# Head sums of two groups issued together, with other tile counts, in an attention stack on one Trainium2 core

## The chip, the cores and the metric

The kernel runs on one core of one Trainium2 chip. The metric is the device time of one execution in microseconds; lower is better. A core has four computing engines that run their own instruction streams and wait for each other through semaphores: TensorE (PE in the profile, its weight loads PEld), VectorE (DVE), ScalarE (ACT) and GpSimd (POOL). SyncE (SP) issues the DMAs. TensorE writes only to PSUM, which this kernel uses as eight banks of 128 partitions by 512 floats; everything else lies in SBUF.

## The reference, cut to what matters

Six attention layers (`D=6`) run over a batch of `B=8` sequences of `L=512` rows with `E=128` features and `H=16` heads of width 8; a gated feed-forward part follows. In each layer the softmax weights are averaged over the heads, a fixed decay is added, and a second softmax is taken:

```python
scores = jnp.einsum('blhd,bmhd->bhlm', q, k) * inv_sqrt_d
w_avg = jax.nn.softmax(scores, axis=-1).mean(axis=1)
new_w = jax.nn.softmax(CSCALE * w_avg + rel[None], axis=-1)
sa = jnp.einsum('blm,bme->ble', new_w, h)
h1 = _ln(h + sa, l1w, l1b)
h2 = _ln(h1, l2w, l2b)
ff = jax.nn.relu(h2 @ w1.T + b1_) @ w2.T + b2_
return (_ln(h2 + ff, l3w, l3b), None)
```

The feed-forward part at the end adds `tlin(gelu(tlin(gelu(tlin(silu(..)*..)))))` of the normalised sum to it, with weights of 512 by 512.

## The kernel before, in words

**Units and steps.** The work is a row of 48 units, one for each layer and batch element (`units`, line 202). A unit has 32 steps (`PAIRS`, line 204). Each step computes two score tiles: 128 rows (32 query rows times 4 heads) by 512 keys. Step `s` of a unit is `lc = s // 8` (a block of 128 query rows), `turn = s // 2 % 4` (four heads of the 16) and `half = s % 2`. Two steps make a `Group` (line 367): four score tiles of the same four heads, whose exponentials lie in one tile `e` of 128 x 4 x 512. The text below counts steps within a unit, 0 to 31, so groups with odd `turn` end at steps 3, 7, 11 and so on.

**One score tile** goes through three engines. TensorE multiplies it into one of six PSUM banks that are used in a ring (`ring`, line 156; `scores`, line 385, one pass in a faster 32-bit format). VectorE reduces it to the negated maximum of each row (`peak`, line 394, `top`). ScalarE takes the exponential with that maximum as bias and sums the rows on the way (`exps`, line 399, `e` and `zs`); after that the bank is free for the score tile six tiles later.

**The sum over heads.** For each group VectorE takes the reciprocal of the row sums (line 408) and GpSimd builds the weights `rp` (line 410). Then `gather` (line 417) multiplies `rp` into `e`: four matmuls, each with 128 x 32 weights and a 512 wide operand, each into its own 32 partitions of one PSUM bank `acc`. They are plain 32-bit matmuls and take two passes, so a group has eight matmul records. The four groups of one `lc` accumulate in `acc`; `mix_exp` (line 425) then reads it on ScalarE into `w`. After that come `mix_turn` (four transposes of `w`, line 432), `mix_decay` (line 437), `mix_values` (line 445) and `mix_end` (lines 453 and 454).

**The order of the work** is written out by hand. `later` maps (step, place) to functions, `at` appends one, `first` puts it ahead. In each step the loop at line 579 issues the two score matmuls, then what is pending for TensorE, then the two maxima, then what is pending for VectorE (GpSimd and DMA issues are called from there), then what is pending for ScalarE, then the two exponentials. Each engine takes its instructions in the order issued. `plan_group` (line 538) places, for a group whose second half is step `s`: `weights` in `s+2`, `gather` in `s+5` ahead of other TensorE work of that step, and for the last turn `mix_exp` in `s+5`, `mix_turn` and `mix_decay` in `s+8`, `mix_values` and `mix_end` in `s+10`. So gathers stand in every even step. The odd steps hold one other piece of TensorE work each: `po` (`mix_values`) in steps 1, 9, 17, 25; the transposes `pt_w` in steps 7, 15, 23, 31 (in step 31 also `pt_h` and `pt_u`, lines 220 and 322, which take two banks of the ring); `pk` and `pq` in 3 and 5; `pf` (`hidden`, line 336) in 11, 13, 19, 21; and `py` (`mlp_out`, line 348, sixteen short matmuls) in 27 and 29. In the steps of `py` VectorE adds the result at once (`mlp_add`, line 355).

**The end.** When the last unit's steps are done, the remaining pieces are mixed into the feed-forward part (`gated_in`, `gated`, lines 606 to 663), which runs over the eight batch elements. There `gated_in(b)` adds the input `x` on GpSimd, issues the load of the next one (line 611), and normalises into the tile `vf`; `gated(b)` writes `sil` (line 633), the hidden tiles in the pool of `e`, and `y`.

**Tiles.** Pools give a number of buffers by tag: `e` 4, `w` 2 (shared with `sil`), `wT` 2, `hT` 2 (shared with `vT`), `x` 3, `rp` 4, `acc` 1.

Of the kernel before, what the change touches and what calls it, by code (L numbers as in the profile page):

```python
# [9 lines left out]
F32 = mybir.dt.float32  # L10
# [7 lines left out]
P = 128  # L18
# [3 lines left out]
QB = 32  # L22
# [7 lines left out]
def attn_stack_then_ffn(ctx: ExitStack, tc: tile.TileContext, a: dict, out: bass.AP):  # L30
    nc = tc.nc
    ctx.enter_context(tc.manual_schedule())
    x = a["x"]
    B, L, E = x.shape
# [4 lines left out]
    LC = L // P  # L39
    FC = F // P  # L40
    HC = HID // P
    NB = P // QB
# [4 lines left out]
    wts = ctx.enter_context(tc.tile_pool(name="wts", bufs=1))  # L47
    state = ctx.enter_context(tc.tile_pool(name="state", bufs=1))
    proj = ctx.enter_context(tc.tile_pool(name="proj", bufs=2))
    epool = ctx.enter_context(tc.tile_pool(name="e", bufs=4))  # L50
    work = ctx.enter_context(tc.tile_pool(name="work", bufs=2))
    small = ctx.enter_context(tc.tile_pool(name="small", bufs=6))
    ps_big = ctx.enter_context(tc.tile_pool(name="ps_big", bufs=6, space=PSUM))
# [39 lines left out]
    x_in = {}  # L93

    def load_x(b, n):
        t = state.tile([P, LC, E], F32, tag="x", name=f"x_{n}", bufs=3)
        nc.sync.dma_start(t, x[b].rearrange("(c p) e -> p c e", p=P))
        return t

# [4 lines left out]
    def load_layer(d):  # L104
        qk = wts.tile([P, 2, E], F32, tag="wqk", name=f"wqk_{d}", bufs=2)
        nc.sync.dma_start(qk, a["wqk"][d].rearrange("t e o -> e t o"))
        w1 = wts.tile([P, F], F32, tag="w1", name=f"w1_{d}", bufs=2)
        nc.sync.dma_start(w1, a["w1t"][d])
        w2 = wts.tile([P, FC, E], F32, tag="w2", name=f"w2_{d}", bufs=2)
        nc.sync.dma_start(w2, a["w2t"][d].rearrange("(c p) e -> p c e", p=P))  # L110
        r = wts.tile([P, len(ROWS), E], F32, tag="rows", name=f"rows_{d}", bufs=2)
        nc.sync.dma_start(
            r.rearrange("p k e -> p (k e)"),
            a["rows"][d].rearrange("k e -> (k e)").partition_broadcast(P),
        )
        rows = {name: r[:, k, :] for k, name in enumerate(ROWS)}
        b2s = wts.tile([P, E], F32, tag="b2s", name=f"b2s_{d}", bufs=2)
        nc.gpsimd.tensor_tensor(b2s, rows["ln2_b"], rows["b2"], ALU.add)
        rows["b2s"] = b2s
        lay[d] = (qk, w1, w2, rows)  # L120
# [69 lines left out]
    def transpose(pt, src):  # L190

        for c in range(LC):
            nc.tensor.transpose(pt[:, c * P : (c + 1) * P], src[:, c, :], ident)  # L193

    def transposed(src, n):
        pt = one([P, L], f"pt_{n}")
        transpose(pt, src)
        return pt
# [7 lines left out]
    class Unit:  # L206
# [12 lines left out]

        def turn_h(self, pt):  # L220
            transpose(pt, self.h[:, :, 0:E])
            self.hT = work.tile([P, L], F32, tag="hT", name=f"hT_{self.n}")
            return lambda: nc.scalar.copy(self.hT, pt)

        def project_k(self):
# [141 lines left out]
    class Group:  # L367
# [38 lines left out]
        def weights(self):  # L406
            r = small.tile([P, NB], F32, tag="r", name=f"r_{self.n}")
            nc.vector.reciprocal(r, self.zs)  # L408
            self.rp = small.tile([P, NB, QB], F32, tag="rp", name=f"rp_{self.n}", bufs=4)
            nc.gpsimd.tensor_tensor(  # L410
                self.rp,
                pick.unsqueeze(1).to_broadcast([P, NB, QB]),
                r.unsqueeze(2).to_broadcast([P, NB, QB]),
                ALU.mult,
            )
# [7 lines left out]
                )  # L423

        def mix_exp(self):
            self.w = work.tile([P, LC, P], F32, tag="w", name=f"w_{self.n}")
            nc.scalar.activation(  # L427
                self.w.rearrange("p c l -> p (c l)"), acc, AF.Exp, scale=1.0 / H
            )
# [31 lines left out]
    PE_, DVE_, ACT_, RING_ = range(4)  # L461
    later = {}

    def at(step, place, fn):
        later.setdefault((step, place), []).append(fn)

    def first(step, place, fn):
        later.setdefault((step, place), []).insert(0, fn)

    def pending(step, place):  # L470
        for fn in later.pop((step, place), ()):
            fn()
# [62 lines left out]
        at(s + PAIRS + 11, DVE_, lambda: un.affine_c(0))  # L535
        at(s + PAIRS + 12, DVE_, lambda: un.affine_c(1))

    def plan_group(gr, s):

        first(s + 2, DVE_, gr.weights)  # L540
        first(s + 5, PE_, gr.gather)
        if gr.turn == STRIPS - 1:
            at(s + 5, ACT_, gr.mix_exp)
            at(s + 8, PE_, gr.mix_turn)
            at(s + 8, DVE_, gr.mix_decay)
            at(s + 10, PE_, gr.mix_values)
            at(s + 10, DVE_, gr.mix_end)
# [6 lines left out]
    def step_ring(s):  # L554
        for fn in later.pop((s, RING_), ()):
            fn()()

    for s in range(-2 * PAIRS, 0):
# [4 lines left out]
        step_rest(s)  # L563
        step_ring(s)

    for u, un in enumerate(obj):
        un.z1 = work.tile([P, LC, E], F32, tag="z1", name=f"z1_{un.n}")
        if u + 2 < B:
            x_in[u + 2] = load_x(u + 2, f"in{u + 2}")
        if un.b == 4 and un.d + 1 < D:  # L570
            load_layer(un.d + 1)
        if u == U - B:
            load_ffn()
            xs = {0: load_x(0, "out0")}
        if u + 2 < U:
            plan_before(obj[u + 2])
        plan_turns(u)
        plan_after(un)
        for pr in range(PAIRS):
            s = u * PAIRS + pr  # L580
            lc, turn, half = pr // 8, (pr // 2) % STRIPS, pr % 2
            if half == 0:
                gr = Group(un, lc, turn)
            peak, exps = gr.scores(half)
            if half == 1:
                plan_group(gr, s)
            pending(s, PE_)
            peak()
            pending(s, DVE_)
            pending(s, ACT_)  # L590
            exps()
            step_ring(s)
# [13 lines left out]
    def gated_in(b):  # L606

        xb = xs.pop(b)
        nc.gpsimd.tensor_tensor(xb, xb, hs[b][:, :, 0:E], ALU.add)
        if b + 1 < B:  # L610
            xs[b + 1] = load_x(b + 1, f"out{b + 1}")
        v = work.tile([P, LC, E], F32, tag="vf", name=f"v_{b}", bufs=1)
        ln = Norm(xb, v, f"f{b}")
        ln.stats(0, LC)
        ln.aggregate()
        ln.centre()
        ln.scale()
        yield
        vT = work.tile([P, L], F32, tag="hT", name=f"vT_{b}")
        pt = transposed(v, f"v{b}")  # L620
        nc.scalar.copy(vT, pt)  # L621
        ready[b] = (xb, vT)

    def gated(b):
        xb, vT = ready.pop(b)
        ahead = gated_in(b + 1) if b + 1 < B else iter(())
        gg = epool.tile([P, HC, L], F32, tag="e", name=f"fg_{b}")
        for o in range(HC):
            sl = slice(o * P, (o + 1) * P)
            p1, p2 = ring([P, L], f"p1_{b}_{o}"), ring([P, L], f"p2_{b}_{o}")  # L630
            nc.tensor.matmul(p1, fw1[:, sl], vT, start=True, stop=True)
            nc.tensor.matmul(p2, fw2[:, sl], vT, start=True, stop=True)
            sil = work.tile([P, L], F32, tag="w", name=f"sil_{b}_{o}")
            nc.scalar.activation(sil, p1, AF.Silu, scale=cols["f_w1s_col"][:, o : o + 1])
            nc.vector.scalar_tensor_tensor(
                gg[:, o, :], p2, cols["f_w2s_col"][:, o : o + 1], sil, ALU.mult, ALU.mult
            )
            yield
        for wt, sc, nm in ((fh1, "f_h1s_col", "h1"), (fh2, "f_h2s_col", "h2")):
            g2 = epool.tile([P, HC, L], F32, tag="e", name=f"{nm}_{b}")  # L640
            for o in range(HC):
                ph = ring([P, L], f"p{nm}_{b}_{o}")
                for c in range(HC):
                    nc.tensor.matmul(  # L644
                        ph, wt[:, c, o * P : (o + 1) * P], gg[:, c, :],
                        start=(c == 0), stop=(c == HC - 1),
                    )
                nc.scalar.activation(g2[:, o, :], ph, AF.Gelu, scale=cols[sc][:, o : o + 1])
                if (nm, o) in (("h1", HC - 1), ("h2", HC - 1)):
                    next(ahead, None)  # L650
                yield
            gg = g2
        po = ring([P, LC, E], f"fo_{b}")
        for c in range(LC):
            for k in range(HC):
                nc.tensor.matmul(  # L656
                    po[:, c, :], gg[:, k, c * P : (c + 1) * P], fw3[:, k, :],
                    start=(k == 0), stop=(k == HC - 1),
                )
        y = work.tile([P, LC, E], F32, tag="z1", name=f"y_{b}")  # L660
        nc.vector.tensor_tensor(y, po, fw3s.unsqueeze(1).to_broadcast([P, LC, E]), ALU.mult)  # L661
        nc.gpsimd.tensor_tensor(y, y, xb, ALU.add)  # L662
        nc.sync.dma_start(out[b].rearrange("(c p) e -> p c e", p=P), y)

    for _ in gated_in(0):
        pass
# [66 lines left out]
```

## Time and profile before

| | |
|---|---|
| median of three runs | 2820.88 us (2820.86 to 2822.2) |
| the profiled execution | 2825.2 us, of which the span of its instructions is 2823.4 us |
| TensorE clock granted | 0.998 of full |
| busy: PE, ACT, DVE, POOL | 2746.7, 2496.5, 2393.9, 1801.2 us |
| time from one unit's first exponential to the next one's, units 3 to 46 | 50.5 to 51.1 us, 51.0 for nearly all |
| from the first exponential of unit 47 to its last | 48.8 us |
| after the last exponential | 2823.4 - 2479.6 = 344 us |

A row of the profile gives line, engine, operation, tiles written and read, shape and count; then busy time in us and the mean of one in ns; then the idle time of the engine just before such instructions and who ended it. In a timeline the first column is the start in us, the second how long the merged row lasted; brackets hold the idle time before it. Busy time of TensorE is counted from pipelined matmuls whose ends are modelled, so the distance from one start to the next says more than a duration.

### The profile page before, as it was taken

The numbers are of one execution on the slowest core, as the hardware profiler recorded it, in microseconds if no ns is written. First come the engines' busy times: TensorE is split into PE (matmuls) and PEld (weight loads), VectorE is DVE, ScalarE is ACT, GpSimd is POOL, SyncE is SP. The second block draws the span as 40 slices with busy tenths as digits, with TensorE's granted clock in tenths as the row PEclk, the third lists the DMA queues.
The fourth block names the chain that finished last, engine by engine and source line by source line (L and its number), as shares of the span: only waits on it lengthen the run. The fifth ranks groups of instructions, "written<-read, shape, count | busy, mean of one in ns | idle before, by whom it ended". The sixth has DMA issues, their size and how long they took to land.

```text
span 2823.4 us, 51628 instructions
## 1 busy us (share of the span) xinstructions
PE 2746.7 (97%) x14944; PEld 1370.0 (49%) x14944; DVE 2393.9 (85%) x5942; ACT 2496.5 (88%) x6845; POOL 1801.2 (64%) x2205
## 2 busy tenths in 40 slices
PE   5999999999999999999999999999999999989999
PEld 2444545445454454454544545445445454445554
DVE  4999999999999999999999999999999999921110
ACT  5999999999999999999999999999999999933232
POOL 4668776776766767767677676676776767633210
PEclk9999999999999999999999999999999999999999
DMA  5555444544544445444454454454564444300000
GB/s 117 114 118 132 93 104 104 112 108 106 111 105 107 97 113 115 110 92 103 105 127 104 93 113 106 103 120 94 117 153 95 102 105 110 78 8 8 15 12 8
DMA packets 133387, 271.06 MB, mean 96 GB/s; under 512 B 39024, under 2 KB 56560, under 8 KB 133104
## 3 DMA queue, kind: packets, MB, share of 16 engines
q1 hardware_dynamic: 131808, 267.73, 42.3%
q8 instruction: 119, 1.95, 0.3%
q14 instruction: 164, 1.34, 0.2%
q10 hardware_dynamic: 1296, 0.03, 0.0%
HBM read 13.86 MB, written 2.10 MB: 6 GB/s over the span
## 4 chain that ended last, share of the span: by engine, by line
PE 47%; ACT 22%; DVE 18%; POOL 6%; issue 5%; DMA 0%; SPq 0%; POOLq 0%; ACTq 0%; DVEq 0%
ACT e L399 19%; DVE top L394 14%; PE ps L385 13%; PE acc L420 12%; PE py L348 6%; PE ph L644 6%; PE po L445 3%; PE pk L229 1%; ACT w L427 1%; POOL z L306 1%; PE pq L238 1%; POOL rs_a L178 1%; POOL z L186 1%; POOL z L181 1%; ACT g L338 1%
## 5 line engine op out<-in xcount | busy, mean ns | idle before, releaser
L399 ACT ACTIVATE e<-ps,top 128x512 f32<-128x512 f32 x3072 | 2134.5, 840 | 23.9 <-DVE top L394 20.4
L394 DVE TENSOR_REDUCE top<-ps 128x1 f32<-128x512 f32 x3072 | 1952.5, 682 | 42.9 <-PE ps L385 35.8
L385 PE MATMUL ps<-ks,qs 128*128 128x512 f32 x3072 | 1240.0, 477 | 34.2 <-ACT e L399 26.0
L399 ACT ACTIVATION_READ_ACCUMULATOR e<-ps,top 128x1 f32 x3072 | 1103.5, 359 | 0.0
L385 PEld LDWEIGHTS ps<-ks,qs 128*128 128x128 f32 x3072 | 495.4, 189 | 888.3 <-ACT e L399 661.6
L420 PE MATMUL acc<-e,rp 128*32 128x512 f32 x6144 | 819.1, 605 | 0.8 <-POOL rp L410 0.3
L410 POOL TENSOR_TENSOR rp<-pick,r 128x128 f32<-128x128 f32 x768 | 308.1, 401 | 549.8 <-DVE r L408 265.8
L420 PEld LDWEIGHTS acc<-e,rp 128*32 128x32 f32 x6144 | 121.0, 108 | 263.1 <-issue 126.5
L278 POOL TENSOR_TENSOR m<-hiq,mask 128x512 f32<-128x512 f32 x192 | 245.2, 1277 | 4.8 <-DMA qs<-m 4.8
L278 POOL TENSOR_TENSOR m<-loq,mask 128x512 f32<-128x512 f32 x192 | 245.1, 1277 | 2.6 <-DMA qs<-m 2.6
L445 PEld LDWEIGHTS po<-h,wT 128*128 128x128 f32 x1536 | 201.0, 191 | 18.9 <-DVE wT L437 1.5
L445 PE MATMUL po<-h,wT 128*128 128x129 f32 x1536 | 202.7, 275 | 0.7 <-DVE wT L437 0.7
L336 PE MATMUL pf<-uT,w 128*128 128x512 f32 x384 | 195.8, 591 | 0.0
L348 PEld LDWEIGHTS py<-w,g 128*128 128x128 f32 x1536 | 186.2, 192 | 10.9 <-ACT vT L621 1.1
L348 PE MATMUL py<-w,g 128*128 128x128 f32 x1536 | 186.9, 275 | 0.8 <-ACT vT L621 0.8
L338 ACT ACTIVATE g<-pf,b_col 128x512 f32<-128x512 f32 x192 | 168.2, 876 | 2.2 <-PE pf L336 2.2
L661 DVE TENSOR_TENSOR y<-fo,fw3s 128x512 f32<-128x512 f32 x8 | 5.5, 692 | 175.8 <-PE fo L656 175.8
L427 ACT ACTIVATE w<-acc 128x512 f32<-128x512 f32 x192 | 134.2, 699 | 22.6 <-PE acc L420 22.6
L662 POOL TENSOR_TENSOR y<-y,x_out 128x512 f32<-128x512 f32 x8 | 10.1, 1265 | 199.7 <-DVE y L661 199.7
L408 DVE RECIPROCAL r<-zs 128x4 f32<-128x4 f32 x768 | 130.9, 170 | 5.7 <-ACT e L399 0.3
L437 DVE TENSOR_TENSOR wT<-pt_w,decay 128x512 f32<-128x512 f32 x192 | 126.9, 661 | 4.5 <-PE pt_w L193 4.2
L355 DVE TENSOR_TENSOR z<-py,z 128x256 f32<-128x256 f32 x96 | 40.8, 425 | 105.3 <-PE py L348 105.3
(97 smaller groups left out, 2637.3 us busy)
## 6 DMA issues: line engine op xcount, KB each, us to landing
qs<-m SPq DMA_DIRECT2D x1536, 128.0 KB, 2.4
ks<-hik SPq DMA_DIRECT2D x384, 64.0 KB, 2.0
ks<-lok SPq DMA_DIRECT2D x384, 64.0 KB, 2.0
rows<-in_rows SPq DMA_DIRECT2D x6, 448.0 KB, 5.1
x_in<-in_x SPq DMA_DIRECT2D x8, 256.0 KB, 3.1
x_out<-in_x SPq DMA_DIRECT2D x8, 256.0 KB, 3.1
out<-y SPq DMA_DIRECT2D x8, 256.0 KB, 2.4
w<-in_w1t SPq DMA_DIRECT2D x6, 256.0 KB, 2.9
```

What stands on the lines that cost most here:

```text
L278: nc.gpsimd.tensor_tensor(m[:, lc - 2 * two], part.unsqueeze(2).to_broadcast([P, NB, PER_STRIP, QB]), mask.unsqueeze(1).to_broadcast([P, N ...
L336: nc.tensor.matmul(pf, w1[:, f * P : (f + 1) * P], self.uT, start=True, stop=True)
L338: return lambda: nc.scalar.activation(self.g[:, f, :], pf, AF.Relu, bias=cols["b1_col"][:, k : k + 1])
L348: nc.tensor.matmul(self.py[:, k, :], self.g[:, f, c * P : (c + 1) * P], w2[:, f, :], start=(f == 0), stop=(f == FC - 1),)
L385: nc.tensor.matmul(ps[s], qs[:, nb * P : (nb + 1) * P].bitcast(F32R), un.ks[:, i, :].bitcast(F32R), start=True, stop=True,)
L394: nc.vector.tensor_reduce(top[s], ps[s], AX.X, ALU.max, negate=True)
L399: nc.scalar.activation(self.e[:, nb, :], ps[s], AF.Exp, bias=top[s], accum_out=self.zs[:, nb : nb + 1],)
L410: nc.gpsimd.tensor_tensor(self.rp, pick.unsqueeze(1).to_broadcast([P, NB, QB]), r.unsqueeze(2).to_broadcast([P, NB, QB]), ALU.mult,)
L420: nc.tensor.matmul(acc[nb * QB : (nb + 1) * QB, :], self.rp[:, nb, :], self.e[:, nb, :], start=(self.turn == 0), stop=(self.turn == STRIPS ...
L427: nc.scalar.activation(self.w.rearrange("p c l -> p (c l)"), acc, AF.Exp, scale=1.0 / H)
L445: nc.tensor.matmul(self.po, self.wT[:, c, :], self.unit.h[:, c, 0 : E + 1], start=(c == 0), stop=(c == LC - 1),)
L644: nc.tensor.matmul(ph, wt[:, c, o * P : (o + 1) * P], gg[:, c, :], start=(c == 0), stop=(c == HC - 1),)
```

## The change

The gathers of two neighbouring groups (turns 0 and 1, or 2 and 3) are held back until the second one's place, and are issued there one behind the other: sixteen matmul records in steps 0, 4, 8 and so on, none in steps 2, 6, 10. `mix_exp` moves from `s+5` to `s+6`. The pool of `e` gets five tiles, `rp` six; `w`, `hT` (with `vT`) get one, `x` two. `v` of the end takes the tag `m0`, `sil` the tag `wT`. The inputs of the end are loaded two at the start of the last layer, then each one after the output of the element two before it.

```diff
-    epool = ctx.enter_context(tc.tile_pool(name="e", bufs=4))
+    epool = ctx.enter_context(tc.tile_pool(name="e", bufs=5))
...
-        t = state.tile([P, LC, E], F32, tag="x", name=f"x_{n}", bufs=3)
+        t = state.tile([P, LC, E], F32, tag="x", name=f"x_{n}", bufs=2)
...
-            self.hT = work.tile([P, L], F32, tag="hT", name=f"hT_{self.n}")
+            self.hT = work.tile([P, L], F32, tag="hT", name=f"hT_{self.n}", bufs=1)
...
-            self.rp = small.tile([P, NB, QB], F32, tag="rp", name=f"rp_{self.n}", bufs=4)
+            self.rp = small.tile([P, NB, QB], F32, tag="rp", name=f"rp_{self.n}", bufs=6)
...
-            self.w = work.tile([P, LC, P], F32, tag="w", name=f"w_{self.n}")
+            self.w = work.tile([P, LC, P], F32, tag="w", name=f"w_{self.n}", bufs=1)
...
-    def plan_group(gr, s):
+    def plan_group(pair, gr, s):
         first(s + 2, DVE_, gr.weights)
-        first(s + 5, PE_, gr.gather)
+        pair.append(gr)
+        if len(pair) == 2:
+            two = tuple(pair)
+            pair.clear()
+            first(s + 5, PE_, lambda: [x.gather() for x in two])
         if gr.turn == STRIPS - 1:
-            at(s + 5, ACT_, gr.mix_exp)
+            at(s + 6, ACT_, gr.mix_exp)
             at(s + 8, PE_, gr.mix_turn)
...
-            xs = {0: load_x(0, "out0")}
+            xs = {b: load_x(b, f"out{b}") for b in range(2)}
...
-        if b + 1 < B:
-            xs[b + 1] = load_x(b + 1, f"out{b + 1}")
-        v = work.tile([P, LC, E], F32, tag="vf", name=f"v_{b}", bufs=1)
+        v = work.tile([P, LC, E], F32, tag="m0", name=f"v_{b}", bufs=1)
...
-        vT = work.tile([P, L], F32, tag="hT", name=f"vT_{b}")
+        vT = work.tile([P, L], F32, tag="hT", name=f"vT_{b}", bufs=1)
...
-            sil = work.tile([P, L], F32, tag="w", name=f"sil_{b}_{o}")
+            sil = work.tile([P, L], F32, tag="wT", name=f"sil_{b}_{o}")
...
         nc.sync.dma_start(out[b].rearrange("(c p) e -> p c e", p=P), y)
+        if b + 2 < B:
+            xs[b + 2] = load_x(b + 2, f"out{b + 2}")
```

More of the change, by code (lines that the diff above doesn't have):

```diff
@@ L564, in attn_stack_then_ffn @@
         step_ring(s)
+    pair = []
     for u, un in enumerate(obj):
@@ L585, in attn_stack_then_ffn @@
             if half == 1:
-                plan_group(gr, s)
+                plan_group(pair, gr, s)
             pending(s, PE_)
```

## The prediction, made before the result was known

> **What bounds the kernel now.** I read the page's busy times and costliest groups first.
>
> ```profile
> PE 2746.7 (97%) x14944; PEld 1370.0 (49%) x14944; DVE 2393.9 (85%) x5942; ACT 2496.5 (88%) x6845; POOL 1801.2 (64%) x2205
> ...
> L399 ACT ACTIVATE e<-ps,top 128x512 f32<-128x512 f32 x3072 | 2134.5, 840 | 23.9 <-DVE top L394 20.4
> L394 DVE TENSOR_REDUCE top<-ps 128x1 f32<-128x512 f32 x3072 | 1952.5, 682 | 42.9 <-PE ps L385 35.8
> L385 PE MATMUL ps<-ks,qs 128*128 128x512 f32 x3072 | 1240.0, 477 | 34.2 <-ACT e L399 26.0
> L420 PE MATMUL acc<-e,rp 128*32 128x512 f32 x6144 | 819.1, 605 | 0.8 <-POOL rp L410 0.3
> L427 ACT ACTIVATE w<-acc 128x512 f32<-128x512 f32 x192 | 134.2, 699 | 22.6 <-PE acc L420 22.6
> L355 DVE TENSOR_TENSOR z<-py,z 128x256 f32<-128x256 f32 x96 | 40.8, 425 | 105.3 <-PE py L348 105.3
> ```
>
> PE looks like the bound at 97%, but those shares mix the attention stack with the end, where ACT and DVE have little to do. Hence one unit of 51 us by itself, from the busy times by stretches (columns: window, span, PE, PEld, DVE, ACT, POOL, clock, DMA share, GB/s):
>
> ```profile
> 1411.25:1462.24 50.99, 50.46 (x293) 25.27 (x292) 48.93 (x123) 49.98 (x142) 36.38 (x45) 1.00 0.54 126
> ```
>
> Three engines stand within 2 us of the period. Next, PE's timeline from step 24 to step 30 of that unit:
>
> ```profile
> 1446.23 0.49 PE L385 MATMUL ps<-ks,qs 128*128 128x512 f32 x1 [0.17 <-ACT e L399]
> 1446.65 1.06 PE L420 MATMUL acc<-e,rp 128*32 128x512 f32 x8
> 1447.65 0.73 PE L385 MATMUL ps<-ks,qs 128*128 128x512 f32 x2
> 1448.22 1.05 PE L445 MATMUL po<-h,wT 128*128 128x129 f32 x8
> 1449.03 0.71 PE L385 MATMUL ps<-ks,qs 128*128 128x512 f32 x2
> 1449.67 1.07 PE L420 MATMUL acc<-e,rp 128*32 128x512 f32 x8
> 1450.66 0.73 PE L385 MATMUL ps<-ks,qs 128*128 128x512 f32 x2
> 1451.23 1.95 PE L348 MATMUL py<-w,g 128*128 128x128 f32 x16
> 1452.93 0.70 PE L385 MATMUL ps<-ks,qs 128*128 128x512 f32 x2
> 1453.57 1.06 PE L420 MATMUL acc<-e,rp 128*32 128x512 f32 x8
> 1454.56 0.73 PE L385 MATMUL ps<-ks,qs 128*128 128x512 f32 x2
> 1455.13 1.95 PE L348 MATMUL py<-w,g 128*128 128x128 f32 x16
> 1456.83 0.71 PE L385 MATMUL ps<-ks,qs 128*128 128x512 f32 x2
> ```
>
> The first row waits for ACT to free a bank: until step 24 the ring holds PE back. From there to step 30 PE never waits. ACT and DVE in the same stretch:
>
> ```profile
> 1454.70 0.60 ACT L427 ACTIVATE w<-acc 128x512 f32<-128x512 f32 x1 [0.47 <-PE acc L420]
> ...
> 1458.23 0.69 ACT L399 ACTIVATE e<-ps,top 128x512 f32<-128x512 f32 x1 [0.25 <-DVE top L394]
> ```
>
> ```profile
> 1453.22 0.42 DVE L355 TENSOR_TENSOR z<-py,z 128x256 f32<-128x256 f32 x1 [0.64 <-PE py L348]
> ...
> 1457.12 0.42 DVE L355 TENSOR_TENSOR z<-py,z 128x256 f32<-128x256 f32 x1 [0.61 <-PE py L348]
> ```
>
> So a unit has two parts. From step 3 to step 27 ACT's starts follow each other without a gap: the exponentials set the pace. Around the two `py` blocks PE sets it. ACT's least time per unit, from the smallest distances between starts: 64 exponentials x 0.664 + 4 `w` x 0.478 + 4 `g` x 0.571 + `qT` 0.571, `kT` 0.587, `hT` 0.466, `uT` 0.676 = 49.0 us. DVE's, likewise (64 maxima x 0.597, the rest about 10.4), is some 48.5. Even if PE cost nothing a unit would keep 49.0 of its 51.0 us.
>
> **What the Trainium skill says.** "TensorEngine Tiling", section Tiling Modes, says that changing the tiling mode drains TensorE. The trace agrees: from the last `acc` start to the next score matmul are 522 ns, where plain passes follow each other in 429; and from a score matmul to `acc` 327, to other work 231. "TensorE: Matmul & The Clock Gate", Part 3, has tiles of one mode start about 4 ns apart; here the four of a pass start 6 to 7 ns apart, so a group costs two passes of 433 + 20 ns. The same page, in its architectural detail, calls ACT and DVE strict FIFO; the `z` rows above show it, for the maxima of the next step stand behind that wait. "Perfetto Trace Analysis", Per-engine timelines, says that a matmul's end is computed; I therefore count starts, and rows such as 0.49 are not used as costs.
>
> **The change, part by part.** *Pairing, on PE.* With a gather between steps 2 and 3 of a pair, from the second score matmul of one step to the second of the next are 327 + 453 + 20 + 522 + 338 = 1660 ns. Without one, where the trace has four score matmuls in a row, about 235 + 230 = 465. So the dropped block saves 1195, and the second group behind the first adds 2 x 453 = 906: 289 ns less PE per pair, 384 x 0.289 = 111 us in all, if PE alone set the time. No trace shows two groups in a row; it could not be under 2 x 433 and not over a separate block, so the pair gains 0 to 0.33.
>
> *Pairing, on the path.* What PE saves in steps 3 to 27 is worth nothing, since the ring stops it anyway. What counts is that one break in the supply of score tiles grows from 1.32 us (score to score) to 2.23. Take step n = 8 or 16, where PE stands at the ring, and t = 0 at the start of the second exponential of step n-3. Score matmuls that wait for the ring start 0.88 to 1.14 after it; I take 0.90, as an idle moment on ACT shortens the lag. First gather +0.43 (the distance after such a wait), then 3 x 0.453 + 0.02 + 0.522 = 1.90: the next score matmul at 3.23. Its maximum starts 0.54 later, at 3.77; DVE has been out of work since about 3.2 (with a single group it would come at 2.86, before that). Then two maxima 1.21, and in the `po` step `r` 0.085, `rw` 0.174, `z` 0.267: the maximum of step n+2 at 5.51, its exponential 0.75 later at 6.26. ACT would have been there after nine exponentials, 5.98. Loss 0.28 us, twice per unit: **+0.56**. With the ends of the lag (0.88 to 1.14, and 0.71 to 0.78 from maximum to exponential) it is 0.2 to 0.5; if DVE has a backlog, 0.
>
> *Around `py`.* From the ring-held score matmul of step 24 (1446.23) to the first of step 30 (1456.83) are 10.60 us with three groups in three blocks, steps 24, 26 and 28. With pairs in 24 and 28 it is four groups in two blocks: + 2 x 0.906 - 1.195 = +0.62. The exponentials of step 30 wait for this today (the 0.25 above), so they come 0.62 later, less about 0.20 for the shorter ring lag. After that, steps 30 to 3, a single pair in step 0 and PE 0.9 earlier at `pk`: ACT's waits there, `kT` 0.32 and two others 0.2, go, and two of about 0.2 come for the maxima behind that pair: -0.13. Together **+0.29**, ends 0 and +0.7.
>
> Per unit +0.85. Units 3 to 46 have the full load: 44 x 0.85 = **+37 us**. Units 0 to 2 and 47 I leave as they are (within 3 us).
>
> *`mix_exp` a step later.* It costs ACT the same 0.478, now behind two more exponentials (1.33) while the pair ends 0.91 later: its 22.6 us of waits mostly go, which is in the sums above. Behind it on ACT stand `g` or `qT` and the exponentials; for it waits `mix_turn` two steps on, where the ring stops PE by more. `acc` is free three steps before the next pair. Cost 0; without the ring's wait up to 0.25 a time.
>
> *Buffers.* Five `e`: the exponentials that reuse a tile come two steps behind its gather (over 2.6 us), as before; with four they would stand behind the pair. `rp` six: likewise nothing. One `w`: read in step s+8, next written in s+14, six steps or 9 us later. One `hT`: written after step 31, last read in 5, 26 steps free. Two `x`: the third was never needed at once in the stack. All 0. *The end:* the load of `x` is now behind the output of the element two before, on SP where nothing else is queued and behind GpSimd's `y`; it takes 3.1 us to land and is first used after 16 + 32 passes of 0.43, some 20 us. `v` in `m0` and `sil` in `wT` meet tiles long read. Cost 0; without that cover up to 6 x 3.1 = 19 us.
>
> **The sum.** The profiled execution took 2825.2 us (span 2823.4), 0.15% over the median of 2820.9; 2825.2 + 37 = 2862, against the median **2858 us**.
>
> **Rivals.**
> 1. *The saved switches reach the end* (faster). If DVE keeps 0.6 us of maxima in hand when a pair begins, it doesn't run dry, and the three pairs around `py` and step 0 give 3 x 0.289 = 0.87 us per unit: 45 x 0.87 = 39 us, **2782**. For it: PE at 97%, and a full ring of six tiles holds 4 us of exponentials, more than the 2.23. Against it: DVE has only what it hasn't yet reduced, and it now runs dry at two blocks that are shorter than a pair (0.64 and 0.61 before `z`). It decides at 0.6 us of backlog on DVE.
> 2. *ACT's floor* (faster still): all of ACT's 2.0 us of gaps per unit go, 45 x 2.0 = 90, **2731**. Against it: two `py` blocks and a pair still stand between steps 26 and 30.
> 3. *A wash*: the losses of steps 8 and 16 equal what the later `mix_exp` and the PE time bring: **2821**.
>
> **Chances.** Slower as worked out 0.60; same 0.10; rival 1 0.20; rival 2 0.10. Faster and slower mean more than 0.2%, about 6 us, what a measurement of this kernel can tell from none. The forecast's own range is 0 to +1.6 per unit: 2821 to 2891. Slower and faster cases both count, so the 8 in 10 reach from 2775 (rival 2 and the lower part of rival 1 left out) to 2890.
>
> **What would show it.** In the trace of after: 384 runs of sixteen `acc` records, passes 433 apart; four score matmuls in a row before each; PE busy per unit down by about 2 us where the period is not. Gaps of DVE of 0.5 us ahead of the first maximum after a pair in steps 9 and 17, gaps of ACT of 0.3 at steps 10 and 18; the exponential of step 30 about a microsecond after its predecessor. I am wrong if DVE has no such gaps, or if the period falls under 51.0. A unit of 50.1 would be rival 1, 49.0 rival 2.

## The result, and the profile after

| | before | after |
|---|---|---|
| median | 2821.19 us (2820.86 to 2822.2, 4 runs) | 2861.86 us (2861.32 to 2863.21, 4 runs) |
| ratio, 95% interval | 1 | 1.0144 [1.0127, 1.0162] |
| profiled execution, its span | 2825.2 us, 2823.4 | 2862.03 us, 2860.2 |
| granted clock | 0.998 | 0.997 |

The change makes the kernel 1.4% slower, 40.7 us by the medians, and 36.8 us between the two spans that the profile shows: the profiled execution before lies 4.0 us above its median, the one after 0.2. From the page after: the busy times, and the costliest groups.

```profile
PE 2700.5 (94%) x14944; PEld 1426.5 (50%) x14944; DVE 2376.9 (83%) x5942; ACT 2511.9 (88%) x6845; POOL 1798.2 (63%) x2205
...
L399 ACT ACTIVATE e<-ps,top 128x512 f32<-128x512 f32 x3072 | 2079.0, 729 | 77.5 <-DVE top L394 68.8
L394 DVE TENSOR_REDUCE top<-ps 128x1 f32<-128x512 f32 x3072 | 1938.8, 682 | 130.9 <-PE ps L385 126.3
L385 PE MATMUL ps<-ks,qs 128*128 128x512 f32 x3072 | 1153.9, 466 | 46.2 <-ACT e L399 36.6
L420 PE MATMUL acc<-e,rp 128*32 128x512 f32 x6144 | 740.1, 599 | 0.0
```

The instructions are the same in number. TensorE is busy for 46 us less, and the kernel is slower: PE's busy share was not what set the time. The last column has what came in its place. VectorE's maxima waited 35.8 us for score tiles before and wait 126.3 now; the exponentials waited 20.4 us for their maxima and wait 68.8. The same unit by itself, in the busy times by stretches (same columns as before):

```profile
1433.06:1484.77 51.71, 49.46 (x293) 26.46 (x293) 48.52 (x123) 50.30 (x142) 36.28 (x45) 1.00 0.53 124
```

A unit takes 51.7 us in place of 51.0. Next PE's timeline from step 24 to step 30, with pairs in steps 24 and 28:

```profile
1468.03 0.51 PE L385 MATMUL ps<-ks,qs 128*128 128x512 f32 x1 [0.17 <-ACT e L399]
1468.47 1.92 PE L420 MATMUL acc<-e,rp 128*32 128x512 f32 x16
1470.32 0.72 PE L385 MATMUL ps<-ks,qs 128*128 128x512 f32 x2
...
1471.69 1.17 PE L385 MATMUL ps<-ks,qs 128*128 128x512 f32 x4
1472.82 2.02 PE L348 MATMUL py<-w,g 128*128 128x128 f32 x16
1474.60 0.71 PE L385 MATMUL ps<-ks,qs 128*128 128x512 f32 x2
...
1479.36 1.18 PE L385 MATMUL ps<-ks,qs 128*128 128x512 f32 x4
```

The pair is there: sixteen `acc` records in a row, and four score matmuls in a row where the single group of step 26 stood. No score tile is produced from 1468.03 to 1470.32, 2.29 us (1.42 before, from 1446.23 to 1447.65). What that does to VectorE in steps 9 and 17, two excerpts of its timeline:

```profile
1445.06 0.42 DVE L247 TENSOR_SCALAR hiq<-qT 128x512 int32<-128x512 int32 x1
1445.88 1.29 DVE L394 TENSOR_REDUCE top<-ps 128x1 f32<-128x512 f32 x2 [0.39 <-PE ps L385]
...
1447.34 0.35 DVE L454 SCALAR_TENSOR_TENSOR z<-po,rw,h 128x128 f32<-128x128 f32 x1
1447.61 1.88 DVE L394 TENSOR_REDUCE top<-ps 128x1 f32<-128x512 f32 x3
...
1458.37 1.29 DVE L394 TENSOR_REDUCE top<-ps 128x1 f32<-128x512 f32 x2 [0.48 <-PE ps L385]
```

VectorE runs dry for 0.39 and 0.48 us, although it still had `hiq` to do in step 9; then `r`, `rw` and `z` stand ahead of the maxima of step 10. In step 25, behind the pair of step 24, it is dry for 0.49. Behind the pairs of steps 12 and 20 it is not idle: there the maxima start 0.85 us after their score matmuls, not the 0.54 of a VectorE that waits for them. To be dry is not yet a loss: behind step 4 VectorE is dry for 0.37 us in both kernels, but the exponentials follow their maxima by more than 2 us there, so ScalarE has work. Next ScalarE, from the last exponential of step 9 to the first of step 10 in that unit, and in step 30 (rows between are left out):

```profile
1447.46 0.80 ACT L399 ACTIVATE e<-ps,top 128x512 f32<-128x512 f32 x1
...
1448.38 0.69 ACT L399 ACTIVATE e<-ps,top 128x512 f32<-128x512 f32 x1
...
1480.76 0.69 ACT L399 ACTIVATE e<-ps,top 128x512 f32<-128x512 f32 x1 [0.96 <-DVE top L394]
```

Starts are 0.664 apart when ScalarE has work; from 1447.46 to 1448.38 it is 0.92, so 0.26 is lost. The view of idle times doesn't list it: the recorded duration (0.80) fills the distance. One has to look at starts.

**Where the time came from.** I number a unit's 64 exponentials from 0, two to a step, measure each from the start of that unit's `uT`, and take the same number of before off that of after. The difference is 0 up to exponential 3. Apart from steps 4, 12, 20 and 28, where `w` now comes behind the exponentials and no longer ahead of them, it changes at these places:

| place | what lies there | change, us |
|---|---|---|
| steps 2 and 3 | +0.11 behind the pair of step 0, then `kT` (no wait any more) | -0.23 |
| step 10 | pair of step 8 | +0.25 |
| step 18 | pair of step 16 | +0.24 |
| steps 26 to 30 | pair of step 24, both `py`, pair of step 28 | +0.46 |
| the unit | 51.71 against 50.99 | +0.72 |

Of the 0.46, 0.25 shows at step 26, as behind the other two pairs; but the exponentials of step 30 wait for PE, so the sum is set by PE's chain from step 24 to step 30.

Over the span: units 3 to 46 take 2276.3 us against 2243.6 (+32.7), units 0 to 2 150.0 against 145.7 (+4.3), unit 47 +0.9, and what lies before the first exponential and after the last -1.1. That is the 36.8.

From the list of waits after, with the columns time, times, longest:

```profile
PE pt_w L193 <- ACT g L338: 47.3, 92, 0.6
```

The waits of `kT` (10.8 us in 43 before) are gone but for the first, of 2.2, and those of `w` (22.6) have no line left. New is `pt_w`: `w` now comes ahead of `g` in the same step of ScalarE, and `pt_w` needs the one bank that `g` still reads (in step 7 it is `qT`: another 23.6 us in 46). The second experiment says what that costs.

### The profile page after: what moved, and what is told of

It is laid out like the page before. It is cut to its first block, busy times and chain, and to the rows that moved or that the text cites. A ratio compares the mean times of both kernels' runs of the same rounds, so it can differ in the third digit from the quotient of the medians.

```text
span 2860.2 us, 51679 instructions
## 1 busy us (share of the span) xinstructions
PE 2700.5 (94%) x14944; PEld 1426.5 (50%) x14944; DVE 2376.9 (83%) x5942; ACT 2511.9 (88%) x6845; POOL 1798.2 (63%) x2205
## 4 chain that ended last, share of the span: by engine, by line
ACT 35%; PE 34%; DVE 22%; issue 8%; POOL 1%; DMA 0%; SPq 0%; POOLq 0%; ACTq 0%; DVEq 0%
ACT e L399 29%; DVE top L394 17%; PE acc L420 10%; PE ps L385 7%; PE py L348 6%; PE ph L648 6%; ACT g L338 2%; ACT w L427 2%; PE po L445 1%; DVE st_b L172 1%; ACT kT L230 1%; DVE wT L437 1%; PE p L635 1%; PE p L636 1%; ACT qT L239 1%
## 5 line engine op out<-in xcount | busy, mean ns | idle before, releaser
L399 ACT ACTIVATE e<-ps,top 128x512 f32<-128x512 f32 x3072 | 2079.0, 729 | 77.5 <-DVE top L394 68.8
L394 DVE TENSOR_REDUCE top<-ps 128x1 f32<-128x512 f32 x3072 | 1938.8, 682 | 130.9 <-PE ps L385 126.3
L385 PE MATMUL ps<-ks,qs 128*128 128x512 f32 x3072 | 1153.9, 466 | 46.2 <-ACT e L399 36.6
L385 PEld LDWEIGHTS ps<-ks,qs 128*128 128x128 f32 x3072 | 527.9, 189 | 652.3 <-ACT e L399 465.4
L399 ACT ACTIVATION_READ_ACCUMULATOR e<-ps,top 128x1 f32 x3072 | 759.2, 247 | 0.0
L420 PE MATMUL acc<-e,rp 128*32 128x512 f32 x6144 | 740.1, 599 | 0.0
L420 PEld LDWEIGHTS acc<-e,rp 128*32 128x32 f32 x6144 | 160.4, 109 | 348.2 <-issue 273.9
L193 PE MATMUL pt_w<-ident,w 128*128 128x128 f32 x768 | 123.3, 283 | 70.9 <-ACT g L338 47.3
L193 PEld LDWEIGHTS pt_w<-ident,w 128*128 128x128 f32 x768 | 84.1, 140 | 130.2 <-ACT g L338 80.9
L338 ACT ACTIVATE g<-pf,b_col 128x512 f32<-128x512 f32 x192 | 135.6, 706 | 2.2 <-PE pf L336 2.2
```

The lines of the kernel that those rows point to most:

```text
L338: return lambda: nc.scalar.activation(self.g[:, f, :], pf, AF.Relu, bias=cols["b1_col"][:, k : k + 1])
L385: nc.tensor.matmul(ps[s], qs[:, nb * P : (nb + 1) * P].bitcast(F32R), un.ks[:, i, :].bitcast(F32R), start=True, stop=True,)
L394: nc.vector.tensor_reduce(top[s], ps[s], AX.X, ALU.max, negate=True)
L399: nc.scalar.activation(self.e[:, nb, :], ps[s], AF.Exp, bias=top[s], accum_out=self.zs[:, nb : nb + 1],)
L420: nc.tensor.matmul(acc[nb * QB : (nb + 1) * QB, :], self.rp[:, nb, :], self.e[:, nb, :], start=(self.turn == 0), stop=(self.turn == STRIPS ...
```

## The experiments

My theory: the pair's longer break in the supply of score tiles costs, since VectorE runs dry behind it. Rivals: the later `mix_exp` (with the new wait of `pt_w`), and the fewer buffers with the two early loads of `x`. Every kernel is an edit of the changed one, unless said otherwise; its ratio is against the kernel before, run beside it.

**1. No pairs, all else as changed.**

```diff
-        pair.append(gr)
-        if len(pair) == 2:
-            two = tuple(pair)
-            pair.clear()
-            first(s + 5, PE_, lambda: [x.gather() for x in two])
+        first(s + 5, PE_, gr.gather)
         if gr.turn == STRIPS - 1:
-            at(s + 6, ACT_, gr.mix_exp)
+            at(s + 5, ACT_, gr.mix_exp)
```

> All of the change except the pairing and the later exponential of the mixture: the buffer counts (five e, six rp, one w, one hT, two x), the shared tags and the later loads at the end stay, each group's sum stands in its own step again and mix_exp in s+5. Theory (the 2.2 us break that a pair makes in the supply of score tiles starves VectorE and then ScalarE): as before, 2821 us, 51.0 us per unit. Rival (a tile count or the end costs the time): it stays near 2862 us.

Measured: 2819.19 us against 2819.44, ratio 1.000 [0.9991, 1.0009]; a unit takes 50.92 (50.99 in the trace of the kernel before, and the 0.07 lie evenly over the unit). The buffer counts, the tags and the loads of the end cost nothing together.

**2. Pairs, `mix_exp` where it was.**

```diff
-            at(s + 6, ACT_, gr.mix_exp)
+            at(s + 5, ACT_, gr.mix_exp)
```

> The change with mix_exp put back into s+5, pairs kept. Theory: the pair ends before ScalarE gets to mix_exp in steps 4, 12 and 20, and in step 28 the wait moves ahead of two exponentials but the exponential of step 30 still waits for TensorE: within 8 us of 2862 us. Rival (the later mix_exp, which puts w ahead of g or qT in one step and lets the transposes pt_w wait about 0.67 us three times per unit, is the cause): most of the 41 us come back, 2825 us or so.

Measured: 2860.09 against 2819.44, ratio 1.0144 [1.0129, 1.0159], the unit 51.69: the whole loss. The wait of `pt_w` on PE is gone, and from step 5 to step 27 every exponential but those next to `w` stands within 0.01 us of its place in the changed kernel, so that wait cost nothing. The ring holds PE instead: PE's waits for it rise from 36.6 to 60.8 us. In step 28 `w` waits for the pair again (53.0 us in all), and by step 30 the two kernels are level. The pairs alone are the cause.

**3 and 4. Which pairs?** A group has a turn from 0 to 3. Pairing only turns 2 and 3 leaves pairs in steps 4, 12, 20 and 28; only turns 0 and 1, in steps 8, 16, 24 and 0. `mix_exp` is at s + 5 in both. The edit of the first; the second has `gr.turn < 2`.

```diff
         pair.append(gr)
-        if len(pair) == 2:
+        if not (gr.turn >= 2):
+            first(s + 5, PE_, gr.gather)
+            pair.clear()
+        elif len(pair) == 2:
```

> Half of the pairs: only turns 2 and 3 are paired (they land in steps 4, 12, 20, 28); turns 0 and 1 stand alone in their own steps; mix_exp in s+5; all buffers as in the change. Theory: in steps 4, 12 and 20 VectorE has a backlog when the pair starts and nothing is lost; from step 24 to 30 there are now three groups in two blocks, 0.34 us less than before the change: 50.7 us per unit, about 2808 us, faster than before the change. Rival (each pair costs the same, 384 pairs for 41 us): half the loss, 2841 us.

Measured: 2815.72 against 2819.44, ratio 0.9989 [0.998, 0.9997], the unit 50.83.

> The other half of the pairs: only turns 0 and 1 are paired (they land in steps 8, 16, 24 and 0), turns 2 and 3 stand alone; mix_exp in s+5; all buffers as in the change. Theory: these are the pairs that start when TensorE stands at the ring; 0.25 us lost at steps 10 and 18, and from step 24 to 30 there are four groups in three blocks, 0.86 us more than before: 51.9 to 52.2 us per unit, 2862 to 2875 us, no better than the full change. Rival (each pair costs the same): half the loss, 2841 us.

Measured: 2907.92 against 2819.44, ratio 1.0314 [1.0297, 1.0331], the unit 52.7.

The split is as I had it: the loss comes with the pairs of steps 8, 16, 24 and 0, and the others together gain a little. Both sizes were off. In the fourth kernel the pairs of steps 8 and 16 cost about twice what they do in the change: 0.24 at step 10 and 0.29 more in step 11, and the same at steps 18 and 19. The pair of step 0 costs 0.12, about as in the change. VectorE and ScalarE in steps 9 to 11 of the fourth kernel (rows between are left out):

```profile
1417.96 1.29 DVE L394 TENSOR_REDUCE top<-ps 128x1 f32<-128x512 f32 x2 [0.49 <-PE ps L385]
```

```profile
1419.56 0.79 ACT L399 ACTIVATE e<-ps,top 128x512 f32<-128x512 f32 x1
...
1420.46 0.69 ACT L399 ACTIVATE e<-ps,top 128x512 f32<-128x512 f32 x1
...
1422.08 0.69 ACT L338 ACTIVATE g<-pf,b_col 128x512 f32<-128x512 f32 x1 [0.17 <-PE pf L336]
```

The first loss is the one known (0.90 from start to start). The second is new: a single group stands in step 10, before PE has caught up, and so `pf` comes late for `g` in step 11. Pairing every group has no such single block. Here a pair followed by a single group is worse than either pattern; this adds to the theory, which had no term for it.

**5 and 6. Without `rw` and `z` behind the pair.** These kernels leave the two instructions out for two strips of four, as the expectation says; the fifth is the changed kernel, the sixth that before with the same edit, as a control.

```diff
     def mix_end(self):
...
+            if lc in (0, 3):
+                nc.gpsimd.tensor_copy(un.z1[:, lc, :], un.h[:, lc, 0:E])
+                return
```

> The change, but VectorE's end of the mixture (reciprocal rw and the update z, 0.44 us) is left out in steps 9 and 17, the steps after the pairs of steps 8 and 16: for those two of the four row blocks of a unit GpSimd copies h into z1 instead, so that part of the attention isn't added. Theory (VectorE has no work in hand when such a pair ends, and the maxima of steps 10 and 18 stand behind rw and z): ScalarE's gaps of 0.25 us in steps 10 and 18 go, 0.5 us per unit, 2862 to about 2840 us. Rival (TensorE's 0.67 us waits for w and g before the transposes are what costs the time): they stay, and so does the time, over 2855 us.

> Control: the same leaving-out (no rw and z on VectorE for the two row blocks whose end falls in steps 9 and 17, GpSimd copies h into z1) in the kernel before the change. Theory: ScalarE has no gaps in that stretch, so less work on VectorE brings nothing there: 2817 to 2821 us. If VectorE's load as such set the time, it would gain as much as the changed kernel does.

Measured: 2846.55 against 2820.94, ratio 1.0091 [1.0076, 1.0106], the unit 51.43; the control 2819.66, ratio 0.9994 [0.9986, 1.0003]. So the two instructions cost nothing before, and with pairs they do: VectorE has no time left behind these pairs. But a unit gains 0.26 us where I expected 0.5 (15 us in all for 22). ScalarE of the fifth kernel from step 9 to step 10, and from step 25 to step 26:

```profile
1438.47 0.80 ACT L399 ACTIVATE e<-ps,top 128x512 f32<-128x512 f32 x1
...
1439.13 0.81 ACT L399 ACTIVATE e<-ps,top 128x512 f32<-128x512 f32 x1
...
1463.00 0.99 ACT L399 ACTIVATE e<-ps,top 128x512 f32<-128x512 f32 x1
...
1464.10 0.69 ACT L399 ACTIVATE e<-ps,top 128x512 f32<-128x512 f32 x1
```

The gap of step 10 is gone (0.66 from start to start), that of step 18 too. In step 26 the distance is 1.10 in place of 0.91. The ring's lag, from an exponential's start to the score matmul that takes its bank, is 1.11 us behind this long unbroken run and 0.89 in the changed kernel, where the gaps interrupt it; the pair of step 24 therefore starts later. Half of what steps 10 and 18 win is lost again there.

**7. A step later for `mlp_add`.** Theory: in the third kernel the `z` that waits for `py` holds up maxima, so a step later would free them.

```diff
-            at(s + step, DVE_, lambda half=half: un.mlp_add(half))
+            at(s + step + 1, DVE_, lambda half=half: un.mlp_add(half))
```

> The pairs of turns 2 and 3 only (as in the third experiment), and in addition mlp_add one step later, so that VectorE takes the two maxima of steps 28 and 30 before it waits for py. Theory: the maximum of step 30 comes 0.43 to 0.54 us after its score matmul rather than 0.34 us after the end of the wait for py, some 0.2 us earlier, and ScalarE waits for it: 50.6 us per unit, about 2806 us. Rival (VectorE's own work, not its order, sets that stretch): as the third experiment, 2816 us.

Measured: 2833.01 against 2820.94, ratio 1.0042 [1.0028, 1.0056], the unit 51.16. A miss, and on the other side. The wait for `py` did leave (77.4 us in the third kernel, 37.5 here, where the first alone is 21.3), and step 30 comes 0.14 earlier than in the third kernel, but then:

```profile
1464.28 0.69 ACT L399 ACTIVATE e<-ps,top 128x512 f32<-128x512 f32 x1 [0.53 <-DVE top L394]
```

That is the exponential of step 31, which didn't wait before. Where it was, `z` fell into time in which VectorE had no tile to reduce anyway; a step later it comes, with `st_c` behind it, while tiles are there. So the waits at `z` that left, 40 us in all, held step 30 up by only 0.14 in a unit, and the later place costs 0.46 more in step 31.

**8, 9 and 10. Where does the gain of the third kernel come from?** The edit is that of the third, with the condition `gr.turn >= 2 and gr.lc == 2` (only the pair of step 28), `gr.turn >= 2 and gr.lc == 3` (only step 4), and `gr.turn >= 2 and gr.lc != 2` (steps 4, 12 and 20).

> One pair per unit instead of eight: only turns 2 and 3 of the third row block, which land in step 28, between the two py blocks; all other groups stand alone, mix_exp in s+5, buffers as in the change. Theory: the pairs of steps 4, 12 and 20 of the third experiment neither cost nor bring anything, its 0.17 us per unit against before come from this pair alone (one break less between steps 24 and 30): again 50.8 us per unit, 2814 to 2818 us. Rival (the saved switching time of every pair counts): only a quarter of that gain is left, 2820 us.

Measured: 2828.43 against 2818.94, ratio 1.0035 [1.0022, 1.0047], the unit 51.09: a miss. The pair between the two `py` blocks costs some 0.17 us per unit against the kernel without pairs. PE in step 27, just before it, and the wait of `w` in the list:

```profile
1452.02 0.50 PE L385 MATMUL ps<-ks,qs 128*128 128x512 f32 x1 [0.17 <-ACT e L399]
```

```profile
ACT w L427 <- PE acc L420: 35.7, 46, 1.1
```

With step 26's block away, PE comes up against the ring in step 27, so what a saved block brings is lost at once; the longer pair then comes late for `w` (26.3 us of waits without pairs). `mix_exp` is in s + 5 here; this pair alone with `mix_exp` a step later was not run. I changed the theory: the gain must be that of step 4. Without a group in step 2, `pk` is about a microsecond earlier and `kT` doesn't wait.

> One pair per unit, turns 2 and 3 of the last row block, which lands in step 4 of the next unit; all other groups alone, mix_exp in s+5, buffers as in the change. Theory as amended after the eighth run (a pair costs where TensorE stands at the ring or between the py blocks; the only one that brings something is that of step 4, since without the sum in step 2 the projection pk comes a microsecond earlier and ScalarE's wait of 0.32 us before kT goes): 50.65 us per unit, about 2807 us. Rival (the gain of the third experiment comes from the pairs of steps 12 and 20, or from all together): 2819 us, as without pairs.

> Three pairs per unit, those of steps 4, 12 and 20; step 28 has none; all else as in the ninth run. Theory: steps 12 and 20 neither cost nor bring anything, so the same time as with the pair of step 4 alone, about 2807 us, within 3 us of that run. Rival (each pair's 0.34 us of saved TensorE time counts for something there): faster than the ninth run by 10 us or more; if those pairs starve VectorE too, slower by 10 us or more.

Measured: 2806.78 and 2806.98 against 2819.95, ratios 0.9954 [0.9941, 0.9966] and 0.9955 [0.9942, 0.9969], units of 50.6. The wait of `kT` in the ninth kernel:

```profile
ACT kT L230 <- PE pk L229: 2.2, 1, 2.2
```

Only the first is left. Exponential by exponential, the ninth kernel is 0.33 ahead of the kernel before from step 3 on and 0.35 ahead at step 28. The pairs of steps 12 and 20 do nothing either way; that of step 28 takes away most of what step 4 brings (third against tenth kernel). One pair of the eight is worth having, and the kernel with that one alone beats both, the kernel before by 0.46% and, by the two ratios, the changed one by 1.9%.

## Why the prediction came out as it did

It gave 2858 us for 2861.86, and its cause was the right one: the pairs alone cost (first and second experiments), and the loss is made where the supply of score tiles breaks for longer than VectorE's stock lasts (third to sixth). Step by step:

- *Pairing, on PE.* Block to next score matmul is 1.854 us where 1.90 was taken: passes start 453, 429 and 429 ns apart, so the second group adds 0.858 and not 0.906. That is even under the 2 x 433 that the prediction held for the least; 433 is the first distance of a block, 453, less the 20 within a pass. So a pair saves 0.34 and not 0.289; the four score matmuls in a row follow as assumed. "TensorEngine Tiling", Tiling Modes, says that a change of mode drains TensorE; one change in and out less is worth this third of a microsecond here, and no run shows how much of it is the drain.
- *Pairing, on the path.* Right in kind and size: lag 0.89 for an assumed 0.90, VectorE dry by 0.39 and 0.48, losses of 0.25 and 0.24 where 0.28 each was worked out. That `rw` and `z` decide is shown by the fifth and sixth kernels: with them left out the nine exponentials last long enough, and both gaps close. What `r` adds was not tried.
- *Around `py`.* The term was too large, 0.29 for a measured 0.23. The chain from step 24 to step 30 grew from 10.61 to 11.33, by 0.72, not 0.62: the two pairs cost 0.09 less than taken, but the `py` block of step 27 ends 0.19 later. Behind four score matmuls its first matmul starts 0.35 us after the last of them, where it was 0.23, and its second 0.18 later, where it was 0.11; its weight loads start late there. The prediction had no term for that. Of the 0.72, 0.46 reached ScalarE: the ring's lag at step 24 shrank from 1.14 us to 0.89, by 0.26 for the 0.20 allowed. Behind step 30 the gain is 0.23, not 0.13: the 0.33 of `kT`, as the ninth kernel shows, less the 0.11 behind the pair of step 0.
- *Units 0 to 2, 47 and the ends.* The units were left as they were, within 3 us; they lose 5.2, and the ends gain 1.1. So the sum, 37 for a measured 36.8, came out right partly by luck: the units from 3 to 46 lose 32.7, and the rest 4.1. Units 0, 1 and 2 lose 2.2, 0.5 and 1.6. Why, I didn't try, and it stays open.
- *`mix_exp` a step later, and the buffers.* 0, shown by the second and first kernels. `pt_w`'s wait was not foreseen, though the prediction named the cover that hides it: the ring stops PE there.
- *The end.* GpSimd waits 10.8 us in three places for the late `x`, so the cover is not whole, but the stretch after the last exponential takes 343.6 us for 343.8 before, and the first experiment has the same waits at no cost.
- *What would show it.* The runs of sixteen, the gaps of VectorE and ScalarE in steps 9, 10, 17 and 18, and the late exponential of step 30 (0.96 us of idle time before it) are all there; the passes are 429 apart. PE's busy time per unit was to fall by 2 us and fell by 1.0. "Perfetto Trace Analysis", Per-engine timelines, says that a matmul's end is computed; here two score matmuls that wait for the ring start 0.67 us apart (1467.36 and 1468.03), and only 0.17 of it is idle, though the next can start 0.23 behind. So part of PE's waits counts as busy, and the busy time doesn't measure what was saved.
- *Rivals.* The first needed 0.6 us of maxima in hand; behind the pairs of steps 8, 16 and 24 VectorE had none. Behind those of steps 12 and 20 it was not idle, but the time saved on PE there brought nothing either (ninth and tenth kernels). The third is refuted by its size. The second, ScalarE's floor of 49.0, no kernel came near: the best unit was 50.6.

## What to carry to other kernels

Where three engines hand tiles round a ring, a batch that saves time on one of them is paid in the length of the break that the others see: before merging two blocks, compare the break with the work that the next engine has in hand at that moment, not with the whole ring. The same merge was worth 0.33 us in one place and cost 0.25 in another, so place merges one by one; here a block is best taken from in front of a result that an engine waits for (`pk`), and left short where the consumer is already nearly dry. And a wait in the list is a cost only if what stands behind it could have run: the wait at `pt_w` was worth nothing, and those at `z` a small part of their length.

## What was not expected of the hardware

- Two groups of column-tiled `acc` passes back to back keep 429 ns from pass to pass right across the boundary (only the first distance of a block is 453): 1.854 us from the first `acc` to the next score matmul, 0.996 for a single group.
- ScalarE's recorded durations grow in an unbroken run of exponentials (0.68 us for the first, up to 1.07 after some 56), while starts stay 0.664 apart. The bank is released later by as much: a score matmul that waits for the ring starts 0.14 us after the recorded end of the exponential that frees its bank, in the kernel before and in the changed one, while its distance from that exponential's start goes from 0.87 to 1.15. A gap of a quarter of a microsecond sets the duration back, and so removing a gap can make the next wait for a bank longer (fifth kernel: 0.89 to 1.11).
- Score matmuls that follow each other start 226 to 341 ns apart, the larger distance behind a break, and 0.63 us apart behind `pk`, `pq` or `pf`; "a matmul" has no one price here.
